# Layer 0 of a four-layer convolution kernel: line stores on another queue, a wider spread of side work, other PSUM banks for g

## The chip, the cores and the metric

The kernel runs on one core of a Trainium2 chip. A core has five engines with a queue of instructions each, which work side by side: TensorE (PE; its weight loads are shown as PEld), VectorE (DVE), ScalarE (ACT), GpSimd (POOL) and SyncE (SP). SBUF is the working memory, PSUM takes the results of TensorE in eight banks, and DMAs move data between SBUF and DRAM. The metric is the time on the device in microseconds (us). The time before is 2857.34 us, the median of 3 runs.

## What is computed

The input x is 1024 x 16 x 16 x 16 in float32. Four layers follow one another, each of the form x + layer(groupnorm(x)):

```python
x = x + _L0_conv_ref(_gn(x), L0_conv_core0, L0_conv_core1, L0_conv_core2)
x = x + _L1_conv_ref(_gn(x), ...)   # 3x3 depthwise, dense 48-128-16, masks
x = x + _L2_conv_ref(_gn(x), L2_conv_filters, L2_conv_bias)
x = x + _L3_conv_ref(_gn(x), ...)   # as layer 1
```

The change touches layer 0 and what runs beside it. Layer 0 multiplies each sample's 4096 values by a matrix given in tensor-train form by three cores:

```python
IN_DIMS = [16, 16, 16]; OUT_DIMS = [16, 16, 16]; RANKS = [1, 16, 16, 1]
res = vector[:, None]
for core in cores:
    r, o, i, k = core.shape
    res_t = res.reshape(bs, r, i, -1)
    new = jnp.einsum('roik,brix->bkox', core, res_t)
    ...
```

## The kernel before

**Samples and phases.** The 1024 samples are two chunks (n = 0, 1) of 512. Layer 0 is done as a dense 4096 x 4096 multiplication of the chunks side by side. Its outer 2 x 2 split uses seven products in place of eight (`OUTER`), one for each of seven phases; a phase has eight units, and in a unit an inner split of seven products (`INNER`) takes two steps each. So a phase is 8 x 14 = 112 steps, and a step is eight matmuls of 128x128 by 128x256 (line 1299). "Step 14" below means the first step of unit 1 of phase 0.

**What a unit does inside its steps** (`pieces`, line 1285). At its steps 5 and 9 it builds weights of the next unit (`build`, line 1218): 32 small matmuls into four banks with the tag w, which ScalarE then copies to SBUF with four copies (line 1231). At 7 and 11 it issues loads of g for the unit after that (`gload`, line 1216, four DMAs on SP into one of three gq buffers). At 2, 4, 6, 12 and 13 VectorE mixes weights (`mix`, lines 1256 and 1258). At step 1 the result of the unit before is stored (`store`, line 1270): r on SP, and, in phase 0, also its negative neg, which ScalarE writes to a t4 buffer and SP stores. Products are gathered from PSUM (three banks with the tag o) by VectorE and ScalarE (lines 1337 to 1347).

**Buffers in question.** The tag t4 has three SBUF buffers of 128x1024 values. In phase 0 they serve g (the pieces' output), lines (two turned lines of the input) and neg; the sums and squares of other phases use them too. PSUM has four w banks, one m bank and three o banks.

**Side work.** Beside its matmuls, phase 0 also does the following.
- `piece` (line 593) computes half of a block of g = core1 x core2: 16 matmuls into two PSUM tiles pg, one on bank m, one on a bank w; four copies by ScalarE (line 605) bring them to a t4 buffer, and after the second half SP stores it to g_dram (line 610). Four pieces are done ahead of steps 1 to 4, the eight others, `rest[4:]`, ahead of steps 16, 19, 22, ... 37.
- `turn` (line 921) transposes one line of the input on TensorE into bank m (ptin), and ScalarE copies it to half of a t4 buffer (line 935). After each second line GpSimd's queue stores the pair to the array xr in DRAM (line 937). Phase 0 turns the 16 late lines of chunk 0 (`lines[1]`). Phase 1 turns the 32 lines of chunk 1 with the same function.
- `make1` prepares layer 1's weights. Its steps are inputs (loads, and memsets on VectorE), dense0, bias_lines, bias_rows and dense1 (small products on bank m), taps (21 small DMAs on GpSimd's queue), order (20 copies by GpSimd and eight DMAs that write zeros to wy, line 357), xpats (line 319 and after), and then 11 folds: each makes a block (eight matmuls into two w banks, four copies by ScalarE into one of three buffers) and sends it with 2 to 16 DMAs of GpSimd (line 402).
- `part_steps(1)` reads the late lines back from xr (line 1059) and prepares the operand of phase 1 on VectorE.

**What sets the order.** All engines keep the order in which the program issues their instructions. `run` (line 1721) issues the steps, and after each step those items of side work whose share of the phase has come: a list with the bounds lo and hi is spread over that part of the steps by the items' costs. A number without a function in it is a pause, in us, of the given total for the phase (215 us); pauses are shortened together when they would take more than 0.7 of the span. `paused` (line 1770) puts such pauses between make1's items. `before` holds what is issued ahead of a step.

Of the kernel before, what the change touches and what calls it, by code (L numbers as in the profile page):

```python
# [20 lines left out]
P = 128  # L21
# [83 lines left out]
def conv_preact_kernel(ctx: ExitStack, tc: tile.TileContext, a: dict, out: bass.AP):  # L105
    nc = tc.nc
    V, A, G, T = nc.vector, nc.scalar, nc.gpsimd, nc.tensor
# [15 lines left out]
    def stage(es, sb, ps):  # L123

        for key, sizes, kw in (("sb", sb, {}), ("ps", ps, {"space": PSUM})):
            p = es.enter_context(
                tc.tile_pool(name=f"{key}{len(pool)}", bufs=1, reuse_waits="tile", **kw)
            )
            pool[key] = p, sizes
        pool[len(pool)] = None  # L130

    def work(shape, tag, name, dt=F32):
        p, sizes = pool["sb"]
        return p.tile(shape, dt, tag=tag, name=name, bufs=sizes[tag])
# [3 lines left out]
    def bank(shape, tag, name):  # L138
        p, sizes = pool["ps"]
        if tag == "mw":  # L140
            either[0] ^= 1
            tag = "mw"[either[0]]
        return p.tile(shape, F32, tag=tag, name=name, bufs=sizes[tag])
# [369 lines left out]
    def train_setup(room, kept_room):  # L513
# [52 lines left out]
        def gmul(pg, h, ih, x, r, q):  # L566
            rows = slice(32 * r, 32 * r + 16)
            T.matmul(
                pg, c1t[rows, h, 2 * ih + x], c2[rows, 64 * q : 64 * q + 64], start=True, stop=True
            )  # L570
# [22 lines left out]
        def piece(q, h, r0):  # L593
            if r0 == 0:
                st0["gl"] = work([P, 2, 4, P], "t4", "g")
            g = st0["gl"]
            pg = [bank([P, 2, 2, 64], tag, "pg") for tag in "mw"]
            for x in range(2):
                for ih in range(2):
                    for r in range(2):  # L600
                        gmul(pg[r][:, x, ih], h, ih, x, r0 + r, q)
            for x in range(2):
                for r in range(2):
                    f = 64 * x + 16 * (r0 + r)
                    A.copy(
                        g.rearrange("p i o f -> p (i o) f")[:, :, f : f + S],
                        pg[r][:, x].rearrange("p i (o j) -> p (i o) j", j=S),
                    )
            if r0 == 2:
                nc.sync.dma_start(  # L610
                    g_dram[h, q].rearrange("p i o f -> p (i o f)"),
                    g.rearrange("p i o f -> p (i o f)"),
                )
# [283 lines left out]
    def input_steps(n, tag, queue):  # L897
# [23 lines left out]
        def turn(h, wh):  # L921
            pt = bank([P, 4, P], tag[0], "ptin")
            for bg in range(4):
                x = slots[:, 4 * (h // 8) + bg].rearrange("p (h w f) -> p h w f", h=8, w=2)
                T.transpose(pt[:, bg], x[:, h % 8, wh], ident)
            pt = pt.rearrange("p g b -> p (g b)")
            if n == 0 and h < 8:
                if h >= 4:
                    A.copy(X[:, 1, 4 * wh + h - 4], pt)
                else:  # L930
                    A.copy(raw[:, 4 * wh + h], pt.rearrange("p (n i) -> p n i", n=2))
                return
            if h % 2 == 0:
                st["l"] = work([P, 2, NB], "t4", "lines")
            A.copy(st["l"][:, h % 2], pt)
            if h % 2 == 1:
                G.dma_start(
                    xr[n][wh, h - 1 : h + 1].rearrange("h p b -> p h b"), st["l"]
                )

# [37 lines left out]
        def kept(b):  # L978
            for wh in range(2):
# [13 lines left out]
        lines = [  # L993
            [
                (1, lambda h=h, wh=wh: turn(h, wh))
                for b in (2 * half, 2 * half + 1)
                for wh in range(2)
                for h in range(4 * b, 4 * b + 4)
            ]
            for half in range(2)  # L1000
        ]
# [10 lines left out]
    def first_normed(b, i):  # L1012

        X, E = part_tile(0)
        cols = slice(256 * i, 256 * i + 256)

        def op(t, k):
            x = X[:, b, t : t + 4, i]
            centre_scale(x, x if b else raw[:, t : t + 4, i], 0, cols, k)

        return [(1.2, lambda t=t, k=k: op(t, k)) for t in (0, 4) for k in range(2)]
# [739 lines left out]
    def steps_of(*more):  # L1761
        return (lambda: None), [x for m in more for x in m]

    def now(steps):
        for step in steps:
            step = step[1] if isinstance(step, tuple) else step
            if callable(step):
                step()

    def paused(xs):  # L1770

        pause = [12, 8, 2, 2, 6, 12, 10, 12] + [2.5] * (len(xs) - 8)
        return [z for x, t in zip(xs, pause) for z in (x, t)]

    L1, make1 = nca_weights("L1_conv_", XN[1][:, 0:16])
    L3, make3 = nca_weights("L3_conv_", XN[1][:, 0:16])
    with ExitStack() as es:
        stage(es, dict(gn, w1=1, w0=2, s2=1, s5=1, r=2, gq=3, R=2, A=1), dict(w=4, m=1, o=3))
        flat = XN[0].rearrange("p n b -> p (n b)")
        sums, cores, early, rest = train_setup(flat[:, 8192:9216], flat[:, 15360:16384])  # L1780
        tag = ["w"]
        loads, stat, lines, tail, (spread0, spread1), kept = input_steps(0, tag, nc.sync)
        now(loads)

        A.activation(work([P, NB], "n", "warm")[:, 0:1], ident[:, 0:1], AF.Sqrt)
        (coefs, gload, build, mix), phases = layer_train()
        now([sums])
        coefs(0)
        now([cores] + stat[0])
        early()  # L1790
        gload(0, 1, G)
        gload(0, 0, G)
        now(lines[0])
        kept(0)
        kept(1)
        gload(1, 0)
        gload(1, 1)
        build(0, 1)
        build(0, 0)
        now(stat[1] + tail[:2])  # L1800
        mix(0, "s2")
        now([spread0] + tail[2:] + [spread1])
        x00, x11, x10, x01 = (first_normed(*at) for at in ((0, 0), (1, 1), (1, 0), (0, 1)))
        now(x00[0::2] + x00[1::2])
        mix(0, "s5")
        now(x11[:2])
        coefs(1)
        tag[0] = "m"
        more = combined(0)
        before = {  # L1810
            1: x11[2:] + rest[0:1],
            2: x10[:2] + rest[1:2] + x10[2:] + more[0:2],
            3: rest[2:3],
            4: rest[3:4] + more[2:4],
            5: more[4:6],
            7: x01,
            8: more[6:8],
            9: more[8:10],
        }
        for i, piece in enumerate(rest[4:]):  # L1820
            before[16 + 3 * i] = [piece]

        def with_operand(i, step):
            return lambda: (now(before.get(i, ())), step())

        phases[0] = [with_operand(i, step) for i, step in enumerate(phases[0])]
        run(
            steps_of(phases[0]), 215, (),
            (lines[1], 0.14, 0.36), (paused(make1), 0.08, 0.64), (part_steps(1), 0.65, 0.97),
        )  # L1830
        loads, stat, lines, tail, more, _ = input_steps(1, tag, G)
        tail += [(0, more[0]), 2, (0, more[1]), 2]
        stat[1] = [[(2.6, s1[1]), s2] for s1, s2 in zip(stat[1][0::2], stat[1][1::2])]
        stat[0] = [[x] for x in stat[0]]
        woven_in = [
            x for j in range(2) for i in range(4) for x in stat[j][i] + lines[j][4 * i : 4 * i + 4]
        ]
        run(
            steps_of(phases[1]), 210, (),
            ([(0, x) for x in loads] + [12] + woven_in + tail, 0.0, 0.6), (part_steps(2), 0.66, 0.97),  # L1840
        )
        run(
            steps_of(phases[2]), 210, (), (paused(make3), 0.02, 0.6), (part_steps(3), 0.62, 0.96),
        )
        run(
            steps_of(phases[3]), 210, (), (part_steps(4), 0.05, 0.9),
            (residual_steps(0, range(S)), 0.1, 0.9),
        )
        run(
            steps_of(phases[4]), 210, (), (part_steps(5), 0.05, 0.9),  # L1850
            ([lambda: conv.update(s=conv_weights()), 60, lambda: conv["s"]()], 0.0, 0.5),
            (residual_steps(1, range(S)), 0.1, 0.9),
        )
        run(steps_of(phases[5]), 210, (), (part_steps(6), 0.05, 0.9))
        nst, N = parts_cw(X0, True, 3)
        bg = alone(N, 0) + alone(N, 1) + alone(N, 2) + rstd(nst, slice(0, 96)) + [3] + scaled(N, range(3))
        run(
            steps_of(phases[6]), 210, load_cw(X0, xf[0]) + [put(L1)], (bg, 0.12, 0.97), by=0.2
        )
# [64 lines left out]
```

## Time and profile before

| What | us |
|---|---|
| Median of the three runs | 2857.34 |
| The runs | 2857.34, 2856.89, 2862.66 |
| The profiled execution | 2862.98 |
| Its span | 2860.9 |
| TensorE busy in the span | 2780.5 |
| Phase 0, from its first matmul to the first of phase 1 | 45.3 to 328.2 |
| Phase 1 | from 328.2 |

Times in the profile are counted from the start of the span of one execution. In a list of groups or waits, `L935` is line 935 of the kernel, and `out<-in` names the tiles. In a list of waits the numbers are the sum in us, how often, and the longest. In a timeline a line gives the start, the duration, and in brackets how long the engine was idle before it and what ended that. In a table of stretches each engine has its busy time and its number of instructions; then follow the granted TensorE clock as a share of full speed, the mean share in which the DMA engines were busy, and GB/s. SPq is SP's queue and POOLq is GpSimd's. Idle time of an engine counts only where the work that ends last waits for it.

### The profile page before, as it was taken

The numbers are of one execution on the slowest core, as the hardware profiler recorded it, in microseconds if no ns is written. First come the engines' busy times: TensorE is split into PE (matmuls) and PEld (weight loads), VectorE is DVE, ScalarE is ACT, GpSimd is POOL, SyncE is SP. The second block draws the span as 40 slices with busy tenths as digits, with TensorE's granted clock in tenths as the row PEclk, the third lists the DMA queues.
The fourth block names the chain that finished last, engine by engine and source line by source line (L and its number), as shares of the span: only waits on it lengthen the run. The fifth ranks groups of instructions, "written<-read, shape, count | busy, mean of one in ns | idle before, by whom it ended". The sixth has DMA issues, their size and how long they took to land.

```text
span 2860.9 us, 47294 instructions
## 1 busy us (share of the span) xinstructions
PE 2780.5 (97%) x19028; PEld 1825.2 (64%) x19028; DVE 1665.6 (58%) x2196; ACT 1232.9 (43%) x2168; POOL 468.1 (16%) x685
## 2 busy tenths in 40 slices
PE   7889999999999999999999999999999999999997
PEld 6667888877888888888888843343333333334344
DVE  8324744732644445444455668757877877767654
ACT  3233232134222112112223256676778657676664
POOL 2442010155011141100000001111112321110000
PEclk8999999999999999999999999999999999999998
DMA  6355744446575577462361145546566867444665
GB/s 233 87 125 182 252 137 143 123 77 133 146 201 113 100 168 176 78 166 60 63 172 38 27 136 112 105 114 160 109 149 134 202 97 189 101 97 105 172 178 203
DMA packets 247114, 383.40 MB, mean 134 GB/s; under 512 B 30292, under 2 KB 140424, under 8 KB 240752
## 3 DMA queue, kind: packets, MB, share of 16 engines
q1 hardware_dynamic: 180816, 249.78, 27.6%
q0 software_dynamic: 65888, 130.46, 26.6%
q8 instruction: 151, 2.47, 0.4%
q14 instruction: 67, 0.55, 0.1%
q10 hardware_dynamic: 192, 0.13, 0.0%
HBM read 211.31 MB, written 173.92 MB: 135 GB/s over the span
## 4 chain that ended last, share of the span: by engine, by line
PE 78%; DVE 3%; ACT 1%; DMA 1%; issue 1%; SPq 0%; DVEq 0%; ACTq 0%
PE po L1299 38%; PE ph L1708 20%; PE po L1537 8%; PE po L1392 5%; PE pw L1229 3%; PE po L1401 1%; PE ptx L1601 1%; DVE u L1549 1%; DMA xn<-xf 0%; DVE xn L677 0%; PE pcnt L1577 0%; PE L_conv_pe L390 0%; PE pr L824 0%; PE pvar L812 0%; DVE flags L1545 0%
## 5 line engine op out<-in xcount | busy, mean ns | idle before, releaser
L1299 PE MATMUL po<-xn,s 128*128 128x256 f32 x3584 | 809.4, 382 | 3.1 <-DVE xn L1010 2.6
L1711 ACT ACTIVATE hid<-ph,pack 128x512 f32<-128x512 f32 (+1 forms) x1040 | 641.2, 684 | 323.9 <-PE ph L1708 261.8
L1299 PEld LDWEIGHTS po<-xn,s 128*128 128x128 f32 x3584 | 675.5, 191 | 110.7 <-issue 8.0
L1299 PE MATMUL po<-xn,w 128*128 128x256 f32 x2688 | 612.4, 382 | 4.1 <-DVE xn L1039 4.1
L1299 PEld LDWEIGHTS po<-xn,w 128*128 128x128 f32 x2688 | 504.0, 190 | 90.0 <-issue 14.9
L1708 PE MATMUL ph<-xn,wq 32*128 32x512 f32 (+1 forms) x3752 | 516.4, 591 | 4.0 <-DVE u L1549 3.6
L1231 ACT COPY w<-pw 128x512 f32<-128x512 f32 x448 | 230.0, 601 | 512.5 <-PE pw L1229 319.2
L1708 PEld LDWEIGHTS ph<-xn,wq 32*128 32x128 f32 x3752 | 234.0, 185 | 230.5 <-issue 209.4
L1256 DVE TENSOR_TENSOR s<-w 128x1024 f32<-128x1024 f32 x224 | 271.2, 1220 | 185.3 <-PE po L1299 184.7
L1708 PE MATMUL ph<-xn,pack 32*128 32x512 f32 x1288 | 281.8, 620 | 7.6 <-DVE u L1549 5.3
L1337 DVE TENSOR_TENSOR r<-r,po 128x512 f32<-128x512 f32 x168 | 115.2, 686 | 284.7 <-PE po L1299 260.6
L1537 PE MATMUL po<-hid,pack 128*32 128x512 f32 (+1 forms) x2080 | 263.1, 599 | 0.7 <-ACT hid L1711 0.5
L1347 DVE TENSOR_TENSOR r<-r,po 128x256 f32<-128x256 f32 x112 | 47.1, 421 | 333.5 <-PE po L1299 333.5
L1343 ACT COPY r<-po 128x256 f32<-128x256 f32 x112 | 41.6, 372 | 451.7 <-PE po L1299 427.6
L677 DVE TENSOR_TENSOR xn<-xn,m 128x1024 f32<-128x1024 f32 x160 | 188.4, 1219 | 36.9 <-ACT m L700 36.9
L1283 POOL DMA_DIRECT2D xf<-r x56 | 69.0, 1366 | 827.1 <-DVE r L1337 469.6
L1549 DVE SCALAR_TENSOR_TENSOR u<-po,pack,xn 128x512 f32<-128x512 f32 (+1 forms) x130 | 96.4, 741 | 160.2 <-PE po L1537 159.2
L1591 POOL DMA_DIRECT2D xf<-u x96 | 82.7, 861 | 641.7 <-DVE u L1589 617.2
L1708 PEld LDWEIGHTS ph<-xn,pack 32*128 32x128 f32 x1288 | 118.1, 188 | 95.1 <-issue 68.5
L1537 PEld LDWEIGHTS po<-hid,pack 128*32 128x32 f32 x2080 | 55.0, 109 | 180.5 <-ACT hid L1711 86.4
L1392 PE MATMUL po<-xn,convw 128*128 128x512 f32 x368 | 163.6, 598 | 0.0
L1229 PEld LDWEIGHTS pw<-R,gq 32*128 32x128 f32 x3584 | 115.5, 189 | 43.2 <-issue 41.2
(191 smaller groups left out, 2376.2 us busy)
## 6 DMA issues: line engine op xcount, KB each, us to landing
xn<-xf SPq DMA_DIRECT2D x96, 512.0 KB, 7.1
wq<-L_conv_wy SPq DMA_DIRECT2D x192, 192.0 KB, 2.9
xf<-r POOLq DMA_DIRECT2D x56, 512.0 KB, 7.3
gq<-g_dram SPq DMA_DIRECT2D x440, 64.0 KB, 3.1
xf<-u POOLq DMA_DIRECT2D x96, 256.0 KB, 4.1
piece<-xb SPq DMA_DIRECT2D x32, 512.0 KB, 4.8
xf<-xr POOLq DMA_DIRECT2D x32, 512.0 KB, 11.8
xf<-conv POOLq DMA_DIRECT2D x64, 256.0 KB, 5.8
```

Of the source, the lines that this page charges most:

```text
L677: V.tensor_tensor(part, part, m().unsqueeze(1).broadcast_to([P, 2, NB]), op)
L1229: T.matmul(pw[r][:, v, i], g[rows, 2 * v + i], R[rows], start=True, stop=True)
L1231: A.copy(w.rearrange("p i b t m -> p (i b t) m")[:, :, 32 * r : 32 * r + 32].rearrange("p k (v o) -> p v k o", v=2), pw[r].rearrange("p v ...
L1256: V.tensor_tensor(t.rearrange("p i t m -> p i (t m)"), x, y, f)
L1299: T.matmul(po, matrix(u, what)[:, i, t], x, start=i == t == 0, stop=i == 1 and t == 3)
L1337: V.tensor_tensor(part, part, po.unsqueeze(1).broadcast_to([P, 2, 256]), ALU.add)
L1392: T.matmul(st["po", h][wh], conv["fw"][:, y], X[:, 16 * wh + h + y - 1], start=y == max(0, 1 - h), stop=y == min(2, S - h),)
L1537: T.matmul(po[32 * j : 32 * j + 32], nca["w1"][:, v], hid[j], start=v == 0, stop=v == 1)
L1549: V.scalar_tensor_tensor(u, po, nca["b1"], X[:, 8 * q + w2, cols(hf)], ALU.add, ALU.add)
L1591: G.dma_start(tile_cw(xf[n], 8 * q + w2), u, accum_op=ALU.add)
L1708: T.matmul(ph, w, x, start=k == 0, stop=k == len(tiles) - 1)
L1711: A.activation(h, ph, AF.Relu, bias=nca["bt"][:, r : r + 1])
```

## The change

Four edits, all of them in placement or in the choice of a queue or bank; the arithmetic is the same.

```diff
@@ piece
-            pg = [bank([P, 2, 2, 64], tag, "pg") for tag in "mw"]
+            pg = [bank([P, 2, 2, 64], "w", "pg") for _ in range(2)]
@@ turn
             if h % 2 == 1:
-                G.dma_start(
+                nc.sync.dma_start(
                     xr[n][wh, h - 1 : h + 1].rearrange("h p b -> p h b"), st["l"]
                 )
@@ phase 0
         for i, piece in enumerate(rest[4:]):
-            before[16 + 3 * i] = [piece]
+            before[14 * (i // 4 + 1) + (1, 4, 8, 12)[i % 4]] = [piece]
...
         run(
             steps_of(phases[0]), 215, (),
-            (lines[1], 0.14, 0.36), (paused(make1), 0.08, 0.64), (part_steps(1), 0.65, 0.97),
+            (lines[1], 0.2, 0.56), (paused(make1), 0.13, 0.64), (part_steps(1), 0.65, 0.97),
         )
```

Both halves of pg now lie in w banks. Line stores are issued by SP, in phase 1 too. The eight later pieces of g come ahead of steps 1, 4, 8 and 12 of units 1 and 2. The late lines are spread over the shares 0.2 to 0.56 of the phase, and make1 begins at 0.13.

## The prediction

> **What bounds the kernel now.** I read the page first (parts 1 and 4), then cut layer 0's first phase into stretches, then asked who TensorE waited for there, then followed the longest wait backwards through ScalarE, the DMA and GpSimd.
>
> ```profile
> span 2860.9 us, 47294 instructions
> ...
> PE 2780.5 (97%) x19028; PEld 1825.2 (64%) x19028; DVE 1665.6 (58%) x2196; ACT 1232.9 (43%) x2168; POOL 468.1 (16%) x685
> ...
> PE 78%; DVE 3%; ACT 1%; DMA 1%; issue 1%; SPq 0%; DVEq 0%; ACTq 0%
> ```
>
> TensorE carries the end. The 80 us in which it is idle (2860.9 - 2780.5), and what it does at a reduced clock, are all there is to gain without removing matmuls. The stretches of phase 0 (unit 0, unit 1, the stall, the rest; columns as in the page, with clock, DMA share and GB/s last):
>
> ```profile
> 45.32:83.38 38.06, 33.91 (x241) 27.74 (x242) 37.59 (x42) 8.52 (x28) 6.48 (x11) 0.95 0.18 45
> 83.38:129.06 45.68, 39.59 (x289) 32.00 (x287) 13.22 (x31) 15.08 (x40) 17.05 (x33) 1.00 0.27 85
> 129.06:152.16 23.10, 12.22 (x80) 10.07 (x80) 2.45 (x2) 4.87 (x15) 12.87 (x37) 0.84 0.86 171
> 152.16:328.16 176.00, 174.26 (x1156) 138.71 (x1157) 91.94 (x96) 63.76 (x130) 49.31 (x88) 0.98 0.54 158
> ```
>
> So 22.9 of TensorE's idle us lie in these 283 us: 4.2, 6.1, 10.9 and 1.7. The waits of TensorE in 80 to 330 us, then ScalarE's longest wait, then the timeline of TensorE around it:
>
> ```profile
> PE ptin L925 <- ACT lines L935: 10.7, 2, 10.4
> PE pg L568 <- ACT lines L935: 3.4, 5, 0.8
> PE po L1299 <- DVE xn L1039: 1.4, 1, 1.4
> ```
> ```profile
> ACT lines L935 <- DMA xf<-neg: 11.2, 1, 11.2
> ```
> ```profile
> 139.86 1.89 PE L1299 MATMUL po<-xn,w 128*128 128x256 f32 x8
> 152.16 1.11 PE L925 MATMUL ptin<-ident,xn 128*128 128x128 f32 x4 [10.42 <-ACT lines L935]
> 153.07 3.62 PE L1299 MATMUL po<-xn,w 128*128 128x256 f32 x8
> 156.62 1.92 PE L1229 MATMUL pw<-R,gq 32*128 32x128 f32 x32
> ```
>
> The transpose ptin has one bank (m). The one before it, a step earlier, was not copied out, because the copy's target, a t4 buffer, was still being read by the store of neg. Why that store was late is in the issues of 134 to 140 us (median us to landing last) and GpSimd's timeline:
>
> ```profile
> L_conv_wy<-xn POOLq DMA_DIRECT2D x8, 96.0 KB, 11.2
> xf<-neg SPq DMA_DIRECT2D x1, 512.0 KB, 15.9
> xr<-lines POOLq DMA_DIRECT2D x1, 512.0 KB, 16.1
> ```
> ```profile
> 127.02 1.63 POOL L335 DMA_DIRECT2D xn<-L_conv_fz  x3
> 128.64 1.49 POOL L937 DMA_DIRECT2D xr<-lines  x2
> 130.13 3.31 POOL L348 COPY xn<-xn 128x18 f32<-128x18 f32 x20
> 133.38 4.81 POOL L357 DMA_DIRECT2D L_conv_wy<-xn  x8
> 138.19 0.74 POOL L937 DMA_DIRECT2D xr<-lines  x1
> ```
>
> Two causes stand here. The line stores sit in GpSimd's order: two of them, ready at 121 and 127, went out at 128.64, behind the 11 us of taps. And the eight zero writes of order (L357, from 133.38) fill the DMA until about 151: whatever was issued beside them, from either queue, took 16 us instead of 3 to 5. With neg, lines and g all in that crowd, the three t4 buffers were gone.
>
> **What the Trainium skill says.** "Trainium Kernel Development and Optimization", Key Constraints: DMAs of the SP, ACT and POOL queues run on the same 16 DMA engines and interleave; several issuers save only issue time. The trace agrees: neg on SP (15.9 us) and lines on POOL (16.1 us) landed equally late beside the zero writes. So the new queue alone takes no store out of a crowd. "TensorE: Matmul & The Clock Gate", Part 1: after an idle window of about 3.4 us the clock halves, and needs as much busy time to return. The trace agrees: 8 matmuls took 3.62 us after the 10.42 us wait and 1.89 us before it.
>
> **Where the steps fall.** Phase 0 has 112 steps; an item at share s runs after step 112s, rounded down. Turn k of 16 moves from 15.7+1.54k to 22.4+2.52k: 22, 24, 27, 29, 32, 35, 37, 40, 42, 45 and so on to 60, where before 31 and 32 and others followed one another. make1's pauses sum to 119 us; a pause of 12 becomes 4.0 steps (4.4 before), an item 0.6, so: inputs 8 to 14, dense0 14 to 19, bias_lines 17 to 22, bias_rows 18 to 23, dense1 20 to 24, taps 23 to 27, order 28 to 32, xpats 32 to 36, first fold 37 to 40, last fold 68 in both. Pieces of g: 15, 18, 22, 26, 29, 32, 36, 40.
>
> **The sum, part by part**, against the profiled execution (2862.98 us, span 2860.9).
> (a) The stall: 10.42 us, if no new wait replaces it.
> (b) The slow clock behind it: ptin 1.11 for 0.60, po 3.62 for 1.89, pw 1.92 for 1.17: 0.51 + 1.73 + 0.75 = 2.99 us.
> (c) The memsets of inputs (VectorE 75.84 to 78.6) now run ahead of the last combination of unit 0, for which TensorE waited 1.42 us at 79.85. Moved behind step 14 they meet an idle VectorE. 1.42 us gained.
> (d) The m bank. Now pg, ptin and the dense transposes share it, and each successor waits for ScalarE: 0.79, 0.79, 0.81, 0.58, 0.68, 0.72, 0.30, 0.72, 0.72, 0.47, and 0.51 for pg beside a build, 7.09 us together. With pg on w and the turns apart, two neighbours remain: turn with bias_lines (step 22, 0.79) and dense1 with turn (24, as the 0.68 row). Gain 7.09 - 1.47 = 5.62 us.
> (e) pg on two w banks: at least 2 steps of 1.79 us after a build (its four copies take 2.05) and one before it (pg's four take 0.77), so hidden; if ScalarE were late, 0.5 us each for eight pieces, 4 us at most; below nothing it can't go. Taken: 0.
> (f) Folds beside builds: make and build in one step (before 65: 0.66 + 0.49; before 37: 0.55; after 51) and make a step before a build (0.42: before 46; after 46 and 60). 2.1 before, 2.0 after: 0.
> (g) 24 line stores leave POOL's queue (0.73 us each, 17.5 us of its 468.1) for SP's at about 0.35 (the L610 row): 8 here, 16 in phase 1, since turn serves both. POOL and SP are not the bound; the landing (3.5 median) stays. The matmuls, copies and DMAs are as many as before. 0.
> Sum: 10.42 + 2.99 + 1.42 + 5.62 = 20.45 us.
>
> **What is late next.** The stall could move. A step is 1.79 us (7.17/4), a build 1.10, a piece 1.04, a turn 0.45, a make 1.0. From 81.96 (83.38 - 1.42, step 14) to taps: 14 x 1.79 + 2 builds + 4 pieces + 3 turns + 2.8 dense + 1.47 = 119.0. Before, taps (116.3) led to zero writes at 133.4, with two line stores (1.49) between: 15.6 us, so now 134.6, and they crowd the DMA for some 17 us, to about 151.5 (neg landed at 151.4 before). Step 32 starts at 127.7 and step 35 at 135.7. By then neg, issued after step 29 (122), has landed, and so have g of step 32 and the lines of 29: that is the difference to before. In the crowd fall the lines of step 35 (issued 138.6, landing about 153) and the gload of step 39, which SP issues behind them; four such issues took 13.72 us there before (138.91), so SP is free at about 153, and g of step 40 and the next lines land at 156 to 157. t4's next users are lines at step 42 (155.9) and neg at 43 (157.5). They fit with 1 to 3 us; were they late by 3, ScalarE would stand, but bank m is next wanted at step 45 (162) and w at 47. On SP behind those stores are gloads wanted 12 steps later and xf stores. xpats holds POOL 18 to 22 us after the zero writes (22.1 before, 18.4 in make3), to 160 to 163; its 16 sends end about 172 plus 3 to land, and make at 49 wants that buffer at 173: 0 to 2 us for ScalarE, most of it hidden. The last sends come about 1 us later to the end of the fold, so do part_steps' loads; VectorE is full from 276 to 328 but idles 4.3 us (1.74 + 0.49 + 2.06) just before, which covers it.
> Unpriced either way: each wait of (d) also breaks the overlap of ptin (0.60 instead of 0.45), 9 times, up to 1.4 us more gain; residues above, up to 4 us less.
>
> **Rivals.**
> R1, the stall is only moved: the zero writes hold a store of 512 KB for 16 us whatever the queue, and ScalarE meets a t4 buffer that isn't free. For it: equal landing on both queues, margins of 1 to 3 us. Against: one turn in 2.5 steps leaves ScalarE some 5 us. Half of (a) and (b) stays: gain 20.4 - 6.7 = 13.7, up to all of it: 7.0. Time 2844 to 2850.
> R2, slower: SP's queue is in order, and a gload that issues into a full DMA (13.72 us for 4 here; 9.79 for 5 at 330.67, in phase 1) holds the line stores behind it, so t4 runs out, ScalarE stops and TensorE with it. One such stop costs 13.4 (a + b); the gain is used up at 20.4 and slower begins at 26.1, so two stops beyond the old one are needed: 20.4 - 2 x 13.4 - 0.5 = -6.9, 2864. For it: 16 stores of phase 1 join a queue with 61 issues of gq. Against: there t4 serves lines alone and TensorE waited 1.2 us in all.
> R3, pg displaces builds: bank rotation makes each piece wait for the build's copies, up to 2.05 us for eight pieces, 16 us: gain 4, no change. Against: 2 steps' distance.
>
> **How the numbers follow.** The forecast, all of 20.4 less 0 to 4 or plus 1.4: 0.63. R1 0.20, R2 0.09, R3 0.05, more than 22 us 0.03. The runs shown are 2857.34, 2856.89 and 2862.66; the profiled execution belongs to the high one. The gain is taken from the median: 2857.3 - 20.4 = 2837. The forecast's own range is 2832 to 2842; reaching over R1 and the spread of the runs, 2831 to 2850. What a measurement can tell from no change is 0.2% (5.7 us): faster 0.63 + 0.19 + 0.03 = 0.85; same 0.06; slower 0.09.
>
> **What would show it.** The idle of TensorE in phase 0 falls from 22.9 to about 6, no wait above 3 us; ptin at 0.60 throughout; no 1.42 wait in unit 0; pg waits for ScalarE gone; lines on SP, POOL's busy time near 450; the zero writes still crowding the DMA for 17 us. A wait of ptin for lines in steps 42 to 47 would speak for R1, of phase 1 for R2, of pw or pg for ScalarE for R3.

## The result, and the profile after

Runs of both kernels, taken together, six each:

| | median us | lowest to highest |
|---|---|---|
| before | 2859.95 | 2856.89 to 2863.42 |
| changed | 2843.5 | 2837.0 to 2848.94 |

The ratio is 0.9941, with a 95% interval of 0.9922 to 0.996: the changed kernel is 16.5 us faster, by 0.6%. A second set on one chip (five runs against nine) gave 2842.1 against 2861.35, ratio 0.9933 (0.9921 to 0.9946). The forecast was 2837, a gain of 20.4. The direction and the places were as forecast, and the gain was four fifths of the forecast in the first set and 19.25 us in the second. The median of 2843.5 lies 1.5 us above the forecast's own range (2832 to 2842) and next to that of rival R1 (2844 to 2850), so the time alone doesn't tell them apart; the profile does. What was forecast of the causes was partly wrong, as the experiments show.

The profiled execution of the changed kernel took 2848.94 us, the highest of its six runs. Its page begins:

```profile
span 2847.2 us, 47308 instructions
...
PE 2781.9 (98%) x19028; PEld 1827.0 (64%) x19028; DVE 1666.2 (59%) x2196; ACT 1232.6 (43%) x2168; POOL 452.2 (16%) x661
...
q1 hardware_dynamic: 187344, 262.36, 28.7%
q0 software_dynamic: 62432, 117.88, 25.5%
```

POOL issues 24 instructions fewer and is busy 452.2 us for 468.1; 12.58 MB (24 stores of 512 KB) have gone from GpSimd's queue q0 to SP's q1. TensorE has as much to do as before. Its stretches in phase 0 (unit 0, then up to step 30, the steps around order and xpats, the rest), to be read beside those of before:

```profile
45.23:84.18 38.95, 38.95 (x241) 31.66 (x242) 35.72 (x34) 8.52 (x28) 0.00 (x0) 0.81 0.12 42
84.18:126.66 42.48, 41.29 (x301) 33.59 (x300) 15.77 (x39) 13.67 (x40) 14.70 (x26) 1.00 0.32 89
126.66:153.76 27.10, 27.10 (x219) 22.78 (x217) 7.84 (x9) 9.65 (x28) 18.50 (x47) 1.00 0.65 121
153.76:308.38 154.62, 153.50 (x1009) 121.90 (x1009) 86.39 (x89) 60.38 (x118) 48.14 (x87) 1.00 0.63 185
```

And all that TensorE waited for from 45 us to the start of phase 1 (the first of these waits ends with the first matmul of phase 0):

```profile
PE po L1299 <- DVE xn L1010: 2.6, 1, 2.6
PE L_conv_pf L296 <- ACT lines L935: 0.7, 1, 0.7
PE L_conv_pe L390 <- ACT w L1231: 0.7, 1, 0.7
PE ptin L925 <- ACT xn L153: 0.5, 1, 0.5
PE po L1299 <- DVE s L1256: 0.5, 1, 0.5
```

The stall of 10.4 us is gone, and so are the waits of pg. In the third stretch, where the stall was, TensorE doesn't stop at all. The first stretch shows something else: TensorE is busy all of the time, but at a granted clock of 0.81 where before had 0.95. So unit 0 took 38.95 us for 38.06.

Where the profiled 13.7 us come from (2860.9 - 2847.2): step 14 to phase 1 took 244.78 us before (83.38 to 328.16) and takes 224.20 (84.18 to 308.38), 20.6 less; ahead of step 14 it is 0.8 more; and from phase 1 to the end of the span it is 2538.8 for 2532.7, 6.1 more. That last term was in no step of the forecast. It is one wait in phase 4 (lines of TensorE's timeline; xf, below, is the array in DRAM that takes layer 0's results):

```profile
1026.11 1.17 PE L1229 MATMUL pw<-R,gq 32*128 32x128 f32 x32
1030.67 10.03 PE L1299 MATMUL po<-xn,s 128*128 128x256 f32 x32 [3.38 <-ACT r L1345]
1040.64 1.17 PE L1229 MATMUL pw<-R,gq 32*128 32x128 f32 x32
```

The wait cost 3.38 us, and the 32 matmuls after it ran 10.03 us in place of the 7.17 that such a group takes elsewhere: 6.2 us. ScalarE could not write r, since the accumulating store of an earlier r had not landed. That store stood on GpSimd's queue behind the 42 small loads of layer 2's weights (L438 to L449). The waits of ScalarE in the changed kernel and then in the kernel before:

```profile
ACT r L1343 <- DMA xf<-r: 19.1, 1, 19.1
```
```profile
ACT r L1343 <- DMA xf<-r: 15.5, 1, 15.5
```

The wait is there in both. At 15.5 us TensorE doesn't notice it; 19.1 is too much. The three stores of r that went out after the loads landed in 11.3 us (median) in the changed kernel, and in 8.2 us before.

### The profile page after: what moved, and what is told of

Its sections match the earlier page's. It is cut to its first block, busy times and chain, and to the rows that moved or that the text cites. A ratio compares the mean times of both kernels' runs of the same rounds, so it can differ in the third digit from the quotient of the medians.

```text
span 2847.2 us, 47308 instructions
## 1 busy us (share of the span) xinstructions
PE 2781.9 (98%) x19028; PEld 1827.0 (64%) x19028; DVE 1666.2 (59%) x2196; ACT 1232.6 (43%) x2168; POOL 452.2 (16%) x661
## 4 chain that ended last, share of the span: by engine, by line
PE 73%; DVE 4%; issue 3%; DMA 2%; POOL 1%; ACT 1%; SPq 0%; DVEq 0%; POOLq 0%; ACTq 0%
PE po L1299 37%; PE ph L1708 17%; PE po L1537 7%; PE po L1392 5%; PE pw L1229 3%; PE po L1401 1%; DMA xn<-xf 1%; PE ptx L1601 1%; DVE xn L677 1%; DVE u L1549 1%; DMA convn<-in_L_conv_filters_dram 0%; PE pcnt L1577 0%; PE L_conv_pe L390 0%; PE pr L824 0%; DMA xf<-r 0%
## 5 line engine op out<-in xcount | busy, mean ns | idle before, releaser
L1299 PE MATMUL po<-xn,s 128*128 128x256 f32 x3584 | 815.3, 384 | 6.5 <-ACT r L1345 3.4
L1299 PEld LDWEIGHTS po<-xn,s 128*128 128x128 f32 x3584 | 679.8, 192 | 115.3 <-issue 7.0
L1299 PE MATMUL po<-xn,w 128*128 128x256 f32 x2688 | 611.0, 382 | 0.0
L1299 PEld LDWEIGHTS po<-xn,w 128*128 128x128 f32 x2688 | 502.8, 190 | 84.8 <-issue 13.6
L1591 POOL DMA_DIRECT2D xf<-u x96 | 82.6, 861 | 640.2 <-DVE u L1589 618.8
L1229 PE MATMUL pw<-R,gq 32*128 32x128 f32 x3584 | 137.2, 286 | 6.5 <-DMA gq<-g_dram 6.2
```

The lines of the kernel that those rows point to most:

```text
L1229: T.matmul(pw[r][:, v, i], g[rows, 2 * v + i], R[rows], start=True, stop=True)
L1299: T.matmul(po, matrix(u, what)[:, i, t], x, start=i == t == 0, stop=i == 1 and t == 3)
L1591: G.dma_start(tile_cw(xf[n], 8 * q + w2), u, accum_op=ALU.add)
```

## The experiments

The yardstick is the time from step 14 to the first matmul of phase 1, read from TensorE's timeline: 244.8 us before, 224.2 after. It leaves out unit 0, whose clock varies, and phase 4. Theory 1 was that of the forecast: the crowd made by the zero writes holds the three t4 buffers. Theory 2: the stores were late because of their place in GpSimd's order.

### Each part alone

The queue alone, the kernel before with:

```diff
-                G.dma_start(
+                nc.sync.dma_start(
                     xr[n][wh, h - 1 : h + 1].rearrange("h p b -> p h b"), st["l"]
```

> The kernel before, with the line stores on SP alone. Measure: the time from step 14 of phase 0 (first po matmul after unit 0) to the first matmul of phase 1, 244.8 us before and 224.2 after, and the longest wait of ptin for ScalarE in it. Theory 1 (the crowd made by the zero writes holds the three t4 buffers): SP doesn't take neg and the lines of step 29 out of the crowd; ptin still waits 6 to 11 us near step 32 and the stretch is 238 to 246 us. Theory 2 (the stores were late because they stood in GpSimd's order): the wait falls below 2 us and the stretch to 229 to 233.

Measured: 233.0 us. No wait above 0.81 us is left from step 14 on. Theory 1 falls here. SP's timeline and GpSimd's, and the landing (last column) of what was issued from 130 to 150 us:

```profile
132.93 0.36 SPq L1281 DMA_DIRECT2D xf<-neg  x1
```
```profile
132.88 4.39 POOL L348 COPY xn<-xn 128x18 f32<-128x18 f32 x20 [2.42 <-DMA xn<-L_conv_fz]
137.21 4.79 POOL L357 DMA_DIRECT2D L_conv_wy<-xn  x8
```
```profile
L_conv_wy<-xn POOLq DMA_DIRECT2D x8, 96.0 KB, 11.0
xf<-neg SPq DMA_DIRECT2D x1, 512.0 KB, 2.8
g_dram<-g SPq DMA_DIRECT2D x1, 512.0 KB, 12.1
```

The crowd is still there (g took 12.1 us). But neg went out at 132.93 instead of 135.50, ahead of the zero writes, and landed in 2.8 us instead of 15.9. Before, ScalarE had waited 4.0 us for g and 0.6 for neg, because t4 buffers were held by line stores that stood behind taps; so neg was 2.6 us late, and that was enough to fall into the crowd. The zero writes also came later here, 2.9 us counted from step 14, because order's copies waited 2.42 us for their loads and took longer; without that delay neg would still have been 1.4 us ahead. The run with the banks alone, below, shows that less is enough: there neg went out at 132.55, 0.5 us ahead of the zero writes, and landed in 2.8 us as well. The queue doesn't take a store out of the crowd: it brought the next one in front of it.

The spread alone, the kernel before with:

```diff
-            (lines[1], 0.14, 0.36), (paused(make1), 0.08, 0.64), (part_steps(1), 0.65, 0.97),
+            (lines[1], 0.2, 0.56), (paused(make1), 0.13, 0.64), (part_steps(1), 0.65, 0.97),
```

> The kernel before, with the late lines and make1 spread as in the change alone; stores stay on GpSimd's queue, pg stays on m and w. Theory 1: the turns no longer stand close together and neg is stored before the zero writes, so the 10 us wait of ptin goes; but line stores stand behind taps, order, xpats and sends, so ScalarE meets unready t4 buffers later: waits of 0 to 8 us in sum at steps 40 to 50; stretch from step 14 226 to 238 us. Theory 2: the stores behind GpSimd's work stay late and the stall stays at about 10 us: 240 to 246.

Measured: 227.9 us, no wait of ptin above 0.5. The stores are on GpSimd's queue as before, so theory 2 falls as well. From 84 to 240 us ScalarE's only wait for a DMA was 4.2 us for the folds' sends, none for t4. This edit moves two things, the turns and make1 with its zero writes; which of the two does it was not tried apart.

Banks and places of the pieces alone, the kernel before with:

```diff
-            pg = [bank([P, 2, 2, 64], tag, "pg") for tag in "mw"]
+            pg = [bank([P, 2, 2, 64], "w", "pg") for _ in range(2)]
...
-            before[16 + 3 * i] = [piece]
+            before[14 * (i // 4 + 1) + (1, 4, 8, 12)[i % 4]] = [piece]
```

> The kernel before, with pg on two w banks and the pieces of g at steps 1, 4, 8 and 12 of a unit alone. Both theories: the waits of pg for ScalarE's lines (3.4 us) and for VectorE (0.6) go, the stall of ptin stays at 8 to 12 us with its slow clock: the stretch from step 14 is 238 to 242 us. If pg displaced builds, waits of pw or pg for w of over 2 us in sum would show.

Measured: 236.9 us. The waits of pg are gone and none for w came. The stall stays, smaller, and for another store (ScalarE's waits from 115 to 165 us, then TensorE's timeline):

```profile
ACT lines L935 <- DMA g_dram<-g: 8.3, 1, 8.3
ACT g L605 <- DMA xr<-lines: 4.2, 1, 4.2
```
```profile
151.48 1.12 PE L925 MATMUL ptin<-ident,xn 128*128 128x128 f32 x4 [6.91 <-ACT lines L935]
```

The chain is as before: 4.2 us for line stores behind taps, then 8.3 us for a buffer whose store is in the crowd. Only the buffer that falls due is now that of g, stored at 136.72 among the zero writes, instead of neg's.

### The crowd moved

The kernel before, with the loop of zero writes taken from `order` and put into `inputs`, ahead of `V.memset(tk, 0.0)`:

```diff
+            for n, pats in enumerate(TRIPLES):
...
+                                G.dma_start(
+                                    wy.rearrange("q g v h s k -> v s (q g) h k")[v, s],
+                                    zero[0:12].unsqueeze(1).broadcast_to([12, S, HID]),
+                                )
             V.memset(tk, 0.0)
```

> The kernel before, with the eight zero writes to wy moved from order to inputs (step 8 in place of 28), nothing else. Theory 1: the crowd moves to about 84 to 101 us of the span, the stall of ptin near step 32 falls below 2 us, a smaller wait of 0 to 4 us may come at steps 17 to 19, and the stretch from step 14 is 230 to 236 us. Theory 2: the line stores still stand behind taps and order, the stall stays over 6 us: 238 to 246.

Measured: 239.5 us, in the range of theory 2, but its stall didn't come: near step 32 no wait is above 0.72 us, though the line stores stand behind taps as before. A smaller stall, of 4.9 us where theory 1 allowed up to 4, came where the crowd now is (L311 is bias_rows; the lines have moved by nine):

```profile
97.20 0.60 PE L925 MATMUL ptin<-ident,xn 128*128 128x128 f32 x4
102.70 2.90 PE L311 MATMUL L_conv_pb<-xn 48*128 48x256 f32 x6 [4.90 <-ACT lines L935]
106.17 1.97 PE L568 MATMUL pg<-cores,xn 16*128 16x64 f32 x16 [0.58 <-DVE xn L314]
```

So the stall of before needed several things at once: line stores held back on GpSimd's queue, a crowd a few us later, and turns and order at the old steps. Taking the stores off that queue, spreading turns and make1, or moving the crowd each broke it there. That there are only three t4 buffers belongs to the account too, but their number was not varied.

### Each part left out

The edit is in each case the one above, the other way round, on the changed kernel.

> The changed kernel with line stores back on GpSimd's queue. Measure as before: step 14 to phase 1, 224.2 us in the changed kernel. Theory 1: the spread does most of the work; what the queue adds is that stores don't stand behind order, xpats and the sends: without it waits of ScalarE for t4 come back at steps 40 to 55, TensorE loses 0 to 8 us: 224 to 232. Theory 2 (the queue is what matters): the stall is back, 236 or more.

> The changed kernel with the old bounds of lines and make1. Theory 1: the crowd meets neg and two line pairs again, ptin waits 5 to 11 us near step 32: stretch 232 to 240 us, and the 1.4 us wait in unit 0 is back. Theory 2: no wait above 2 us, 224 to 228.

> The changed kernel with pg on banks m and w and the pieces at the old steps. Both theories: waits of pg for ScalarE come back, fewer than before since the turns are apart: 1 to 4 us, no stall: 225 to 229 us.

| Parts in the kernel | step 14 to phase 1, us | less than before | without the slow clock at a fold |
|---|---|---|---|
| none (before) | 244.8 | | 244.8 |
| queue | 233.0 | 11.8 | 231.3 |
| spread | 227.9 | 16.9 | 226.2 |
| banks | 236.9 | 7.9 | 236.9 |
| queue, banks | 227.9 | 16.9 | 226.2 |
| spread, banks | 226.2 | 18.6 | 224.5 |
| queue, spread | 226.3 | 18.5 | 226.3 |
| all | 224.2 | 20.6 | 224.2 |

Alone the three gain 36.6 us in sum, together 20.6: the stall with its clock, 13.4 us, can be removed only once. Theory 2 expected the stall without the queue, theory 1 without the spread; neither came.

The last column takes out an event that some executions have and others don't. Two profiles of the changed kernel gave 224.2 both times, two of the next kernel, which is the same in this stretch, 224.2 and 225.9. The difference lies at the one fold that shares a step with a build (TensorE's timelines of the next kernel's two profiles; L390 is the fold's matmuls, and L1302 was L1299):

```profile
180.77 1.54 PE L390 MATMUL L_conv_pe<-xn 9*36 9x512 f32 x8 [0.66 <-ACT w L1234]
182.25 1.99 PE L1302 MATMUL po<-xn,w 128*128 128x256 f32 x8
```
```profile
179.14 1.54 PE L390 MATMUL L_conv_pe<-xn 9*36 9x512 f32 x8 [0.66 <-ACT w L1234]
180.62 2.71 PE L1302 MATMUL po<-xn,w 128*128 128x256 f32 x8
```

In the second one the steps behind the fold run at a granted clock of 0.50 for a while and lose 1.7 us in all. The same happened in the profiles with the queue alone, the spread alone, with queue and banks, and with spread and banks (1.7 us each). That last one is the changed kernel with the queue left out. Counted from step 14 it starts its builds within 0.01 us of the changed kernel up to this fold; besides the clock it lost 0.3 us there, in a build of 1.62 us for 1.17. So beside the other two parts the new queue gains 0.3 us at most, while leaving out the spread or the banks costs 2.0 or 2.1 us. Alone, the queue removes the stall with its clock (13.5 us), and the spread removes more (18.6 us). Each row is a single profile.

### The wait of phase 4

On the changed kernel, layer 2's loads in groups of four, spread over the phase:

```diff
-            ([lambda: conv.update(s=conv_weights()), 60, lambda: conv["s"]()], 0.0, 0.5),
+            (
+                [lambda: conv.update(s=conv_weights())]
+                + [lambda i=i: conv["s"][1](i) for i in range(0, 42, 4)]
+                + [12, lambda: conv["s"][0]()], 0.0, 0.7,
+            ),
```

> The changed kernel with the 42 small loads of layer 2's weights, which held GpSimd's queue for 27 us in phase 4, spread in groups of four over 0.7 of the phase. In the profile of the changed kernel ScalarE then waited 19.1 us for a buffer r whose accumulating store stood behind them, TensorE waited 3.38 us and ran its next 32 matmuls in 10.03 us for 7.17. Theory 3 (those 6.2 us are what the changed kernel gave back): the wait of ScalarE for xf from r in phase 4 is below 5 us, TensorE doesn't wait there, phase 1 to the end is 2532 to 2533 us in place of 2538.8. Rival: TensorE's time there is set by the clock or the DMA's load, and it stays above 2536.

Measured: ScalarE doesn't wait for xf from r there at all, TensorE doesn't wait from 900 to 1300 us, and phase 1 to the end is 2532.1 us. Two further profiles with the same edit, of the runs below, have no such wait either, while nine of the eleven without it do. That the loads on GpSimd's queue make ScalarE wait is shown by this. The sum of 2532.1 alone wouldn't show it, as the second profile of the changed kernel will. Then it was timed beside the changed kernel:

> The changed kernel once more, as the yardstick for the next two on the same chip. Theory 3 says its runs differ by two events that aren't tied to the change: a slow clock at the start of phase 0 (2 to 3 us) and TensorE's wait in phase 4 for a buffer r (up to 6 us); so its times spread over 2836 to 2849 us, ratio to the kernel before 0.992 to 0.996.

> The changed kernel with layer 2's small loads spread over phase 4, timed. Theory 3: the upper runs of the changed kernel go, the median is 2 to 5 us below that of the changed kernel, the lowest run is equal. Rival (the spread between runs has another cause): same median and same spread.

| | median us | lowest to highest | ratio to before |
|---|---|---|---|
| changed | 2842.10 | 2839.41 to 2848.21 | 0.9933 (0.9921 to 0.9946) |
| with loads spread | 2840.77 | 2839.09 to 2843.11 | 0.9928 (0.9916 to 0.9941) |

The lowest runs agree. The highest fell by 5.1 us, as the theory has it, but the median by 1.3 only, and the intervals overlap: a gain isn't shown by five runs. The second profile of the changed kernel explains why. There ScalarE waited 16.0 us for r and TensorE 0.2 (2530.2 us from phase 1 to the end), and the stores of r landed in 8.4 us, so the 6 us are lost in some executions only.

### The clock ahead of phase 0

As the run before, with matmuls of the identity in TensorE's gaps:

```diff
+        def warm(n):
+            pt = bank([P, 4, P], "w", "idle")
+            for k in range(n):
+                T.transpose(pt[:, k % 4], ident, ident)
...
+        warm(36)
         build(0, 1)
         build(0, 0)
...
-        now([spread0] + tail[2:] + [spread1])
+        now([spread0] + tail[2:])
+        warm(7)
+        now([spread1])
+        warm(9)
```

> As the run before, with 36, 7 and 9 matmuls of the identity that nothing reads, put where TensorE is idle ahead of phase 0, so that its clock isn't lowered. If the slow clock at the start costs time: step 14 begins at 81 to 82 us in every run in place of 81 to 84, the median falls by 0 to 3 us more. Rival: VectorE's preparation of unit 0 sets that time, no gain.

Measured: median 2842.01 (2837.81 to 2842.39), ratio 0.9928 (0.9914 to 0.9941): no gain. TensorE's waits from 45 to 100 us (L1302 was L1299):

```profile
PE po L1302 <- DVE xn L1042: 4.4, 2, 3.2
```

Step 14 came at 82.6 us. The slow clock at the start was gone (the first eight matmuls took 1.99 us for 3.78), but VectorE's combinations set the time of unit 0, and a faster TensorE waits for them. The wait of 3.2 us then lowered the clock again: the 32 matmuls after it took 8.86 us for 7.17, and without these 1.7 us step 14 would have come at 80.9. So the rival stands for the waits, and the warming lost at the last one what it had won.

### The crowd doubled

The changed kernel with:

```diff
-                            for s in slots(n, i):
+                            for s in slots(n, i) * 2:
```

> The changed kernel with each of the eight zero writes of order issued twice (same result, double the crowd, about 34 us in place of 17). Theory 1 (crowd and three t4 buffers make the stall): stores of steps 35 to 45 land 15 to 30 us late, ScalarE waits for t4, TensorE stands 4 to 20 us and the stretch from step 14 to phase 1 is 229 to 246 us in place of 224. Rival (the crowd doesn't matter once stores are on SP and the turns are apart): below 226 us.

Measured: 245.8 us; TensorE stands 16.7 us. The size is as expected and the way isn't: the stores of 139 to 175 us landed in 6 to 10 us (medians), not 15 to 30. ScalarE's waits from 100 to 240 us, and TensorE:

```profile
ACT xn L396 <- DMA L_conv_wy<-xn: 22.1, 1, 22.1
```
```profile
195.83 2.55 PE L1229 MATMUL pw<-R,gq 32*128 32x128 f32 x28 [16.69 <-ACT xn L396]
```

It is the fold, not t4. ScalarE's copy of a fold waits for its buffer, which the sends of three folds earlier still read; these sends stand on GpSimd's queue behind the zero writes and xpats; and a build waits for the w banks that the fold holds. For t4 ScalarE waited only 3.0 us (neg), with no wait of TensorE. So in the changed kernel the crowd no longer reaches TensorE through t4 first, and its weakest place is the fold buffer.

## Why the prediction was right, and where it wasn't

**(a), (b), the stall and its clock: right.** Both are gone, 13.4 us, and nothing took their place in phase 0 of the profiled execution. TensorE stood 2.3 us in the whole phase, where about 6 were forecast; the rest was taken up by the slow clock of unit 0, see (c). R1 and R3 gave no sign: no wait of ptin for lines in steps 42 to 47, none of pw or pg for w. R2 could have shown in phase 1 of every kernel with the new queue: TensorE waited there 1.2 us for ptin, as before.

**(c), the memsets: right in kind, and got in five profiles of nine.** The 1.42 us wait is absent from every kernel with inputs behind step 14, and back without the spread, as expected there. From first matmul to step 14 the kernels with the old place took 38.1 us (four of them; 39.9 with the queue alone, after a longer slow clock). Of nine profiles with the new place five took 36.4, so the gain there was 1.7 us. But in the profiled execution the slow clock lasted through the first three steps and the unit took 38.95; and three took 38.1, among them the second profile of the changed kernel, because of this (TensorE's timeline):

```profile
70.75 1.17 PE L1229 MATMUL pw<-R,gq 32*128 32x128 f32 x32
74.90 8.86 PE L1299 MATMUL po<-xn,w 128*128 128x256 f32 x32 [2.98 <-DVE xn L1039]
```

The clock was lowered after the wait of 2.98 us (8.86 us for 7.17), which cost the 1.7 us again. The forecast had no term for the clock in unit 0.

**(d), the m bank: right.** In the stretch from step 14 the priced terms are 10.42 + 2.99 + 5.62 = 19.03 us, and 20.58 were measured. The two neighbours left in place waited 0.72 and 0.47 us, 1.19 for the 1.47 allowed, so (d) gave 5.90 us. The rest of 1.27 fits the up to 1.4 us named for the broken overlap of ptin, which was not measured on its own. One of the eleven waits, 0.58 us, was for VectorE and not for ScalarE as (d) has it; it went as well.

**(e), (f), (g): right at 0** as far as TensorE's waits show: one fold beside a build cost 0.66 us at step 51 as it had at 65, and the banks alone brought no wait for w. What (f) didn't see is the clock: this fold costs another 1.7 us in some executions, six of the fourteen profiled, though in neither profile of the changed kernel. (g) was also right that the queue adds next to nothing beside the rest, as the table shows.

**"What is late next": the sequence right, a landing mis-sized, the slack in the wrong place.** SP and GpSimd around the crowd, and the landings of what was issued from 140 to 147 us:

```profile
141.25 0.37 SPq L937 DMA_DIRECT2D xr<-lines  x1
142.10 12.68 SPq L1216 DMA_DIRECT2D gq<-g_dram  x4
154.88 0.53 SPq L610 DMA_DIRECT2D g_dram<-g  x1
155.51 0.38 SPq L937 DMA_DIRECT2D xr<-lines  x1
157.50 0.36 SPq L1281 DMA_DIRECT2D xf<-r  x1
160.56 0.36 SPq L1281 DMA_DIRECT2D xf<-neg  x1
```
```profile
140.45 4.79 POOL L357 DMA_DIRECT2D L_conv_wy<-xn  x8
```
```profile
L_conv_wy<-xn POOLq DMA_DIRECT2D x8, 96.0 KB, 10.6
xr<-lines SPq DMA_DIRECT2D x1, 512.0 KB, 6.2
gq<-g_dram SPq DMA_DIRECT2D x3, 64.0 KB, 12.2
```

The gload did hold SP for 12.7 us with g and lines behind it, as forecast from the 13.72 of before. The zero writes began at 140.45, not 134.6: step 14 was 2.2 us later, and order's copies waited 2.12 us for their loads and took 4.19 us for 3.31. The line store of step 35 landed in 6.2 us; some 14 were assumed. So t4 had more room than the 1 to 3 us forecast, and the doubled crowd showed that the fold, which the text gave 0 to 2 us, comes first. In the second profile of the changed kernel ScalarE waited 4.4 us there, in two parts, with no wait of TensorE.

**The step on the queue failed.** "So the new queue alone takes no store out of a crowd" and R1's equal landing on both queues were read rightly from the profile and led to a wrong conclusion: the queue alone removed the stall. What was missed is the order ahead of the crowd. The waits of 4.0 and 0.6 us for line stores were the first link, and neg missed the gap in front of the zero writes by 2.1 us (135.5 against 133.4). The forecast names the line stores held behind taps as one of two causes, but follows only the other. (The first of the two was ready at 119.6, not at 121: its second copy ended then.) It is luck that this error left the sum as it was: the spread was in the change too, and it removes the stall with or without the queue.

**The sum stopped at phase 1.** It took everything after it as unchanged. In the profiled execution 6.2 us were given back in phase 4, by a wait of ScalarE that both kernels have: at 15.5 us TensorE doesn't see it, at 16.0 it waits 0.2, at 19.1 it waits 3.38 and its clock is lowered. Five executions of the second set lie between 2839.4 and 2848.2, which fits the same loss in one of them, but only one of them has a profile: that this is the whole of the spread was not shown. Why the stores of r landed late and the wait was 19.1 us once, and 14.3 to 16.1 in the other profiles that show it, stays open.

**The baseline** was the median of three runs, 2857.3; with six it is 2859.95, so the gain is 16.5 us in the first set and 19.25 in the second, for 20.4. That the second is so near is in part luck: more than was priced from step 14 on, less ahead of it, and a loss after phase 1 that some executions have.

## What to carry to other kernels

Follow a stall back past the store that released it, to what made that store start when it did: a store late by 2.6 us may land 13 us later because of what it ran into. Where a stall needs several coincidences, each of several edits removes it, and their gains alone must not be added; leave each out of the whole to see what it is worth, and compare the timelines step by step: here 1.7 us of a passing slow clock looked like the worth of an edit that gained 0.3 us at most beside the others. After a stretch has become faster, look for waits elsewhere that were just covered before, as phase 4's was at 15.5 us.

## What the runs showed of the hardware

The granted clock came back after very different times at the start of phase 0. In the kernel before the first eight matmuls took 3.78 us and the next 1.99; in the changed kernel the slow clock lasted over three steps, from 45.2 to some 60 us, with TensorE busy all of the time. The Trainium skill, "TensorE: Matmul & The Clock Gate", Part 1, gives about 3.4 us of sustained work for the return and says that it varies from run to run; here it was about 4 us once and 15 another time, so the measurement goes far beyond the page's figure. The times fall into three groups: in the thirteen profiles that start slow the clock came back at or near the end of the first group of eight po in seven, of the second in four and of the third in two. Between the groups stand the matmuls of 16 rows by 64 columns (pg), 1.97 us at the slow clock; that they delay the return would fit, and wasn't tried. With matmuls of the identity ahead (the run on the clock) there was no slow group.

Short idle times lowered the clock. Ahead of unit 0's last combination TensorE waited, after a build, 2.37 to 2.73 us in five profiles and kept full speed (2.72 before), and 2.91, 2.98 and 3.17 us in three, and each time the next 32 matmuls took 8.86 us for 7.17. So in this place the limit lay between 2.73 and 2.91 us, below the 3.4 us of idle time that the prediction quotes. And at the fold beside a build TensorE is idle for 0.66 us or less, within 3.3 us of small matmuls (32 rows, then 9), and the clock was lowered after it in six of fourteen profiles. Whether matmuls of few rows count as idle there is not shown.

Eight zero writes of 96 KB each, from 12 partitions, filled the DMA for some 17 us (133 to 150 us before), at 56 to 238 GB/s in all, while line stores of 512 KB alone land in 3 to 4 us. A store among them took 6.2 us in one kernel and 16 in another; which other transfer made the difference wasn't tried. A store issued 0.5 us ahead of them (the banks alone) took 2.8 us.
